# Reordering the down product of a gated feed-forward block: all high parts first, then all low parts

## The chip, the cores and the metric

The kernel runs on one core of a Trainium2 chip. The metric is the time of one execution on the device in microseconds, and the time given for a kernel is the median of its runs. Besides, one execution is recorded by the hardware profiler, and all timelines below are from that one. The engines are named as in the profile: PE (TensorE, matrix products; PEld is its load of the stationary operand), DVE (VectorE), ACT (ScalarE), POOL (GpSimd) and SP (SyncE, which here issues DMAs).

## The reference

One transformer layer over 4 x 2048 = 8192 tokens of 256 numbers, float32: chunked linear attention with a decay and a gate, then a gated feed-forward part with integer weights. Each part is added to its input and normalized.

```python
Q, K, V = x @ W_q.T, x @ W_k.T, x @ W_v.T          # chunks of 32 tokens
S = einsum('bncd,bnkd->bnck', Qc, Kc) * mask       # decay ** (i - j), lower triangle
O = einsum('bnck,bnkd->bncd', S, Vc)
x = layernorm(x + (sigmoid(x @ W_g.T) * O @ W_o.T + x))
h = silu(x @ wg.T) * (x @ wu.T)                    # 768 wide, integer weights / 127
x = layernorm(x + h @ wd.T)
```

## The kernel before

**Tiles.** The 8192 tokens go in 16 blocks of 512 (`TB`), each of four groups of 128 tokens (`NG` = 4). A PSUM bank holds 512 float32 numbers for each partition, that is two groups of 256 features. Eight banks are handed out in turn by `bank(name)`; a bank is free again when its last reader is done.

**Parts.** Products that need more than one pass's precision are split. In the attention part, `token_parts` cuts a tensor into `hi` (ACT), `lo` (POOL: `x_lo` is x minus its high part) and `gap`, which is made later, by `x_gaps()` on DVE: two instructions (line 477), one for each half of the features. `three` (line 524) multiplies hi and lo parts, has ACT scale the bank in place (line 531), and multiplies the gap parts on top. In the feed-forward part the activations `u` are cut into `u_hi` (fp32r, cast on ACT, line 904) and `u_lo` (float16, POOL, line 905), and the integer weights lie ready as `fd_hi` (fp32r) and `fd_lo` (float16). The hidden dimension of 768 is six chunks of 128.

**The down product.** `ffn_down` (line 922) multiplies u by the down weights. For the blocks b = 0 to 12 it calls `project_back`, 48 products of 128 x 128 by 128 x 256: for each of the four groups six high products (one for each chunk) and six low ones, all into the group's half of a bank. `back_terms` turns the order round in every second group, so PE runs high, low, low, high, high, low, low, high. When a bank's two groups are done, `finish`, here `residual` (line 930), is called: DVE adds h to the bank (line 933) and takes the statistics for the norm (`moments`, lines 336 and 337). The last blocks take another path (`chunkwise`, line 953, and line 1313).

**The order of the work.** Every instruction here is issued through `in_turn`: on each engine the instructions run in the order in which the program names them. So where a call stands in the program sets its place in each engine's queue. The loop over b (from line 1101) works on three blocks at once: the feed-forward part of b, the attention output of b + 2, the attention projections of b + 3. Around the down product the order is: PE ends the output product of block b + 2 (`p_o`); DVE adds x to it and takes its statistics (`st_a`, `mv_a`); ACT makes the high part of the next x (`x_hi`), then loads the table for the square root, makes `rstd_h` and, from the block before, `rstd_out` (line 345), and loads the table of silu again; POOL makes `x_lo`. Then comes `ffn_down` with `between`, a function that makes the scale and shift of the norm of h on DVE (`scale_and_shift`, lines 384 to 387: a reciprocal, two multiplications, `minus_h` and `scale_h`, and `shift_h`) and then calls `x_gaps()`. `residual` calls it once, behind the first bank's statistics. After that DVE takes the reciprocal for `rstd_out`.

The next turn of the loop begins with ACT normalizing h (line 424, needs `shift_h`), PE with the gate and up products of chunk 0 (`fg`, `fu`, line 879), ACT with silu of it (`s`, line 888), DVE with `u` (line 899), then four 32 x 32 transposes `sq` (line 831), which 16 DMAs on SP's queue bring to `hT`. PE goes on with chunk 1, the products `p_y` (line 490) of the next x, chunk 2 and the gap products of `p_y`; DVE copies them to `yT` (line 556), and PE takes `yT` in the scores `ps` (line 652).

Of the kernel before, what the change touches and what calls it, by code (L numbers as in the profile page):

```python
# [54 lines left out]
P = 128  # L55
# [4 lines left out]
NG = TB // P  # L60
# [16 lines left out]
def kernel(  # L77
# [15 lines left out]
    nc = tc.nc  # L93
    NT, D = x.shape
# [19 lines left out]
    def in_turn(ins):  # L114
        tc.keep_in_program_order(ins)

    def bank(name):
        return psum.tile([P, TB], F32, tag="ps", name=name)
# [73 lines left out]
    for n in WARM:  # L192
        nc.tensor.matmul(
            pi[:, :n],
            lhsT=nc.const_aps.tensor(0.0, [P, P]),
            rhs=nc.const_aps.tensor(0.0, [P, n]),
            start=True,
            stop=True,
# [129 lines left out]
    def no_moments(name):  # L328
        return small.tile([P, NG, 2], F32, tag="mv", name=f"mv_{name}")

    def moments(r, name, groups=range(NG), order=free, mv=None):

        mv = no_moments(name) if mv is None else mv
        for g in groups:
            st = small.tile([P, 6], F32, tag="st", name=f"st_{name}_{g}")
            order(nc.vector.bn_stats(st, r[:, g, :]))
            order(nc.vector.bn_aggr(mv[:, g, :], st))
        return mv
# [38 lines left out]
    def scale_and_shift(mv, std, kind, name, eng=nc.gpsimd, order=free):  # L377

        on_r, on_dst = kind
        scale, minus, shift = (  # L380
            small.tile([P, NG], F32, tag=tag, name=f"{tag}_{name}")
            for tag in ("scale", "minus", "shift")
        )
        in_turn(nc.vector.reciprocal(std, std))
        for t, sign in ((minus, -1.0), (scale, 1.0)):
            order(eng.tensor_scalar(t, std, sign * on_dst / on_r, None, ALU.mult))
        order(eng.tensor_tensor(shift, mv[:, :, 0], minus, ALU.mult))  # L387
        return scale, shift
# [326 lines left out]
                )  # L715
        return goT

    def back_terms(g, parts, ws):


        pairs = list(zip(parts, ws))[:: -1 if g % 2 else 1]
        return [term for part, w in pairs for term in zip(part, w)]

    def project_back(b, parts, ws, finish, name):


        per = TB // D
        for h in range(NG // per):
            pb = bank(f"{name}_{b}_{h}")
            for j in range(per):  # L730
                g = h * per + j
                terms = back_terms(g, parts, ws)
                for i, (part, w) in enumerate(terms):
                    product = nc.tensor.matmul(  # L734
                        pb[:, j * D : (j + 1) * D],
                        lhsT=part[:, g * P : (g + 1) * P],
                        rhs=w,
                        start=(i == 0),
                        stop=(i == len(terms) - 1),
                    )  # L740
                    in_turn(product)
            finish(slice(h * per, (h + 1) * per), pb)

    def chunked(t):
        return [t[:, k, :] for k in range(t.shape[1])]

    def flat(t, gs):
        return t[:, gs, :].rearrange("p g d -> p (g d)")
# [167 lines left out]
    def early_and_late(parts, ws):  # L916


        hi, lo = (list(zip(part, w)) for part, w in zip(parts, ws))
        return hi[:-2] + lo[:-2], hi[-2:] + lo[-2:]  # L920

    def ffn_down(b, uT, h, between=None, chunkwise=False, amid=None):


        r = work.tile([P, NG, D], F32, tag="r2", name=f"r2_{b}")
        mv = no_moments(f"f{b}")
        made = None
        order = in_turn

        def residual(gs, pb):  # L930

            order(
                nc.vector.scalar_tensor_tensor(
                    flat(r, gs), pb, SCALE**2 / U_UP * H_UP, flat(h, gs), ALU.mult, ALU.add
                )
            )
            nonlocal made
            moments(r, f"f{b}", range(gs.start, gs.stop), order, mv)
            if between is not None and gs.start == 0:
                made = between()  # L940

        ws = [chunked(w) for w in fd]
        if chunkwise:
            per = TB // D
            banks = [bank(f"fdn_{b}_{k}") for k in range(NG // per)]
            for late, terms in enumerate(early_and_late(uT, ws)):
                if late and amid is not None:
                    made = amid()
                for k, pb in enumerate(banks):
                    for i, (part, w) in enumerate(terms):  # L950
                        for j in range(per):
                            g = k * per + j
                            product = nc.tensor.matmul(  # L953
                                pb[:, j * D : (j + 1) * D],
                                lhsT=part[:, g * P : (g + 1) * P],
                                rhs=w,
                                start=late + i + j == 0,
                                stop=True,
                                skip_group_check=True,
                            )  # L960
                            in_turn(product)
                    if late:
                        residual(slice(k * per, (k + 1) * per), pb)
        else:
            project_back(b, uT, ws, residual, "fdn")
        return r, mv, made

    def store(b, r, start=None):
# [4 lines left out]
    def finish(b, r, start=None):  # L973
        layer_norm(r, f"f{b}", on_r=H_UP)
        store(b, r, start)
# [107 lines left out]
    def up_with_cast(b, hT, uT, hc, kind, pieces):  # L1083

        multiply = ffn_up(b, hT, uT, range(hc, hc + 1), held=True)
        if b == 0:
            cast_fd(kind, pieces)
        multiply()

    uT_0 = [], []  # L1090
    mv = out_rest(lambda: up_with_cast(0, hTs[0], uT_0, 0, 0, range(2)))
# [9 lines left out]
    for b in range(NB - 2):  # L1101
# [7 lines left out]
        uT = ([], []) if b else uT_0  # L1109
# [57 lines left out]
        if more:  # L1167
# [15 lines left out]
            def between():  # L1183
                scales = scale_and_shift(
                    mv_h, std_h, of_h, f"h_{b}", nc.vector, in_turn
                )
                if m + 1 < NB:
                    x_gaps()
                return scales

            r_out, mv_out, scales_h = ffn_down(b, uT, hs.pop(b), between)
            if b:
                scales_out = scale_and_shift(mv_before, std_before, of_out, f"out_{b}")
        else:
# [8 lines left out]
            def amid():  # L1203
                return iterated_scale_and_shift(out_rest(), (HALF, 1.0), f"h_{n}")

            r_out, mv_out, scales_h = ffn_down(
                b, uT, hs.pop(b), chunkwise=True, amid=amid
            )
# [6 lines left out]
    per = NG // 2  # L1215
    cols = [slice(i * per * P, (i + 1) * per * P) for i in range(2)]
    uT_last = [], []
    uT = [], []
# [28 lines left out]
    up(last, uT_last, 0, 1)  # L1247
    no_more_splits()
    r_before, mv_before, _ = ffn_down(last - 1, uT, hs[last - 1], chunkwise=True)
    scales_out = iterated_scale_and_shift(mv_before, of_out, f"out_{last - 1}")  # L1250
    up(last, uT_last, 1, KH - 3)
# [3 lines left out]
    for i in range(per):  # L1255
        ffn_up(last, hTs[last], uT_last, range(KH - 2 + i, KH - 1 + i), cols[0])
        g = per + i
# [31 lines left out]
    r = work.tile([P, NG, D], F32, tag="r2", name=f"r2_{last}")  # L1289
# [17 lines left out]
    banks = [bank(f"fdn_{last}_{g}")[:, :D] for g in range(NG)]  # L1307
# [263 lines left out]
```

## Time and profile before

| What | Value |
|---|---|
| median of 3 runs | 489.17 us (489.13 to 489.43) |
| the profiled execution | 489.44 us |
| its span in the profile | 487.8 us |
| granted clock of PE | 0.999 |
| down product of one block (line 734), b = 0 to 12 | 5.43 us, 48 products |
| from one down product to the next | 23.91 us |
| PE, busy share of the span | 99% |
| ACT, DVE, POOL, busy share | 77%, 69%, 58% |

A line of a timeline gives start and length in microseconds, the engine, the line of the kernel, the operation, output <- inputs (buffer numbers left out), the form of output and input, and how many like instructions are taken together. Matrix products overlap, so the length of such a group is more than the distance to the next. A row of stretches gives, behind the stretch and its length, the busy time of each engine with its number of instructions, the granted clock, and the DMA's share and rate.

### The profile page before, as it was taken

How to read it: one execution, taken by the hardware profiler on the slowest of the kernel's cores; microseconds unless marked ns; L12 is line 12 of the kernel's file. 1: busy time of each engine (PE TensorE's matmuls, PEld its weight loads, DVE VectorE, ACT ScalarE, POOL GpSimd, SP SyncE). 2: the span in 40 equal slices, each digit the busy share in tenths (PEclk: the TensorE clock that was granted, in tenths of full speed). 3: DMA queues.
4: the chain of work that ended last, by engine and by line, in shares of the span. 5: the costliest groups of instructions: out<-in, count | busy, mean ns of one | idle time of the engine just before them, and what ended most of it. 6: DMA issues, size and time to landing. Idle time of an engine off the chain costs nothing.

```text
span 487.8 us, 12289 instructions
## 1 busy us (share of the span) xinstructions
PE 481.4 (99%) x4760; PEld 382.3 (78%) x4760; DVE 338.7 (69%) x795; ACT 374.5 (77%) x699; POOL 281.2 (58%) x285
## 2 busy tenths in 40 slices
PE   9999999999999999999999999999999999999995
PEld 5787787887868878687887868878687887868674
DVE  4687958687575876757677575875757677567656
ACT  4878687687877878688687877878688787786845
POOL 3835755555735565464555735566465555657764
PEclk9999999999999999999999999999999999999999
DMA  8820411211403123131411403123132211103102
GB/s 258 253 92 7 131 45 51 80 46 42 133 22 110 44 59 118 31 101 54 118 47 39 134 25 110 45 80 94 27 105 54 79 44 38 53 20 112 35 14 83
DMA packets 43323, 36.99 MB, mean 76 GB/s; under 512 B 4864, under 2 KB 39168, under 8 KB 43264
## 3 DMA queue, kind: packets, MB, share of 16 engines
q1 hardware_dynamic: 42144, 35.28, 24.4%
q10 hardware_dynamic: 1120, 0.92, 0.6%
q8 instruction: 38, 0.62, 0.5%
q14 instruction: 21, 0.17, 0.1%
HBM read 20.45 MB, written 8.39 MB: 59 GB/s over the span
## 4 chain that ended last, share of the span: by engine, by line
PE 98%; DMA 1%; DVE 0%; ACT 0%; issue 0%
PE fg L879 18%; PE fu L879 18%; PE fdn L734 14%; PE p_v L512 9%; PE p_o L512 9%; PE p_y L490 9%; PE p_g L490 9%; PE po L688 4%; PE ps L652 2%; PE fdn L953 2%; PE fdn L1313 1%; PE pg L576 1%; DMA wg<-in_w_gT_dram 1%; PE pa L767 1%; PE pv L618 1%; PE py L597 1%
## 5 line engine op out<-in xcount | busy, mean ns | idle before, releaser
L905 POOL TENSOR_TENSOR u_lo<-u,u_hi 128x512 f16<-128x512 f32 (+1 forms) x98 | 129.4, 1325 | 96.5 <-ACT u_hi L904 95.4
L899 DVE SCALAR_TENSOR_TENSOR u<-fu,s 128x512 f32<-128x512 f32 (+1 forms) x98 | 66.1, 675 | 84.7 <-ACT s L888 82.5
L888 ACT ACTIVATE s<-fg 128x512 f32<-128x512 f32 (+1 forms) x98 | 57.4, 585 | 48.1 <-PE fg L879 48.1
L904 ACT CAST u_hi<-u 128x512 fp32r<-128x512 f32 (+1 forms) x98 | 59.4, 606 | 32.8 <-DVE u L899 32.8
L879 PE MATMUL fg<-hT_hi,fg_hi 128*128 128x512 f32 (+1 forms) x196 | 72.4, 451 | 0.0
L879 PE MATMUL fu<-hT_hi,fu_hi 128*128 128x512 f32 (+1 forms) x196 | 60.5, 390 | 0.0
L879 PE MATMUL fg<-hT_lo,fg_lo 128*128 128x512 f16 (+1 forms) x196 | 58.2, 379 | 0.0
L879 PE MATMUL fu<-hT_lo,fu_lo 128*128 128x512 f16 (+1 forms) x196 | 57.5, 375 | 0.0
L471 POOL TENSOR_TENSOR go_lo<-goT,go_hi 128x512 fp32r<-128x512 f32 x30 | 44.6, 1506 | 18.2 <-ACT go_hi L470 18.2
L477 DVE SCALAR_TENSOR_TENSOR go_gap<-go_hi,goT 128x512 fp32r<-128x512 f32 x30 | 48.2, 1645 | 0.8 <-ACT go_hi L470 0.7
L471 POOL TENSOR_TENSOR x_lo<-xT,x_hi 128x512 fp32r<-128x512 f32 x30 | 37.8, 1283 | 14.6 <-ACT x_hi L470 14.6
L734 PE MATMUL fdn<-fd_hi,u_hi 128*128 128x256 f32 x312 | 44.6, 285 | 0.0
L879 PEld LDWEIGHTS fg<-hT_hi,fg_hi 128*128 128x128 f32 x196 | 35.7, 190 | 10.3
L879 PEld LDWEIGHTS fu<-hT_hi,fu_hi 128*128 128x128 f32 x196 | 36.6, 188 | 8.4
L788 DVE TENSOR_TENSOR h<-p_o,x 128x512 f32<-128x512 f32 x30 | 19.3, 685 | 32.8 <-PE p_o L512 28.9
L734 PEld LDWEIGHTS fdn<-fd_hi,u_hi 128*128 128x128 f32 x312 | 38.9, 188 | 0.3
L734 PE MATMUL fdn<-fd_lo,u_lo 128*128 128x256 f16 x312 | 38.6, 274 | 0.0
L856 POOL TENSOR_TENSOR hT_lo<-hT,hT_hi 128x512 f16<-128x512 f32 x28 | 35.4, 1284 | 4.3 <-ACT hT_hi L855 4.3
L879 PEld LDWEIGHTS <-fu_lo 128*128 128x128 f16 x196 | 19.2, 98 | 22.2
L734 PEld LDWEIGHTS <-u_lo 128*128 128x128 f16 x312 | 28.4, 98 | 3.9
L424 ACT ACTIVATE h<-h,shift_h,scale_h 128x256 f32<-128x256 f32 x52 | 27.0, 589 | 2.2 <-DVE shift_h L387 0.8
L879 PEld LDWEIGHTS <-fg_lo 128*128 128x128 f16 x196 | 13.1, 98 | 19.2 <-issue 12.8
(175 smaller groups left out, 1042.7 us busy)
## 6 DMA issues: line engine op xcount, KB each, us to landing
x<-in_x_dram SPq DMA_DIRECT2D x16, 512.0 KB, 3.9
xT<-in_xT_dram SPq DMA_DIRECT2D x15, 512.0 KB, 4.7
hT<-sq SPq DMA_DIRECT2D x224, 32.0 KB, 1.9
out_dram<-r SPq DMA_DIRECT2D x13, 512.0 KB, 3.3
out_dram<-r SPq DMA_DIRECT2D x7, 128.0 KB, 1.7
fg_int<-in_ffn_gT_dram SPq DMA_DIRECT2D x3, 256.0 KB, 7.9
fu_int<-in_ffn_uT_dram SPq DMA_DIRECT2D x3, 256.0 KB, 7.1
fd_int<-in_ffn_dT_dram SPq DMA_DIRECT2D x3, 256.0 KB, 5.9
```

The source lines that it names most:

```text
L424: nc.scalar.activation(r[:, g, :], r[:, g, :], AF.Identity, bias=shift[:, g : g + 1], scale=scale[:, g : g + 1],)
L471: in_turn(nc.gpsimd.tensor_tensor(lo[:, k, :], t[:, k, :], whole, ALU.subtract))
L477: nc.vector.scalar_tensor_tensor(gap[:, k, :], whole, -WHOLE, t[:, k, :], ALU.mult, ALU.add)
L490: nc.tensor.matmul(pb, lhsT=a[kind][:, k, i * P : (i + 1) * P], rhs=b[kind][:, k, :], start=kind + k == 0, stop=True, skip_group_check=True,)
L512: nc.tensor.matmul(pb[:, j * D : (j + 1) * D], lhsT=b[kind][:, k, g * P : (g + 1) * P], rhs=a[kind][:, k, :], start=kind + k + j == 0, sto ...
L734: product = nc.tensor.matmul(pb[:, j * D : (j + 1) * D], lhsT=part[:, g * P : (g + 1) * P], rhs=w, start=(i == 0), stop=(i == len(terms) - 1),
L856: nc.gpsimd.tensor_tensor(in_order[1], whole, in_order[0].bitcast(F32), ALU.subtract)
L879: product = nc.tensor.matmul(pb, lhsT=w[kind][:, dc, hc * P : (hc + 1) * P], rhs=hT[kind][:, dc, cols], start=(kind == kinds[0] and dc == ...
L888: in_turn(nc.scalar.activation(s, pg, AF.Silu, scale=SCALE / H_UP))
L899: nc.vector.scalar_tensor_tensor(u, pu, U_UP / H_UP, s, ALU.mult, ALU.mult)
L904: in_steady_turn(nc.scalar.copy(hi, u))
L905: in_steady_turn(nc.gpsimd.tensor_tensor(lo, u, hi.bitcast(F32), ALU.subtract))
```

## The change

`project_back` opens both banks at once. It runs chunk by chunk over the high parts of all four groups (24 products), then the low parts of the first bank (chunk by chunk, two groups each), then those of the second bank. When all 48 products stand, it calls `between()`, and only then `finish` for the two banks. `back_terms` is gone. In `ffn_down`, `begin` takes the place of the call inside `residual`. So on DVE the scale and shift of h and the two differences of x come ahead of both residuals and their statistics; before, they stood between the two.

```diff
-    def back_terms(g, parts, ws):
-        pairs = list(zip(parts, ws))[:: -1 if g % 2 else 1]
-        return [term for part, w in pairs for term in zip(part, w)]
-
-    def project_back(b, parts, ws, finish, name):
+    def project_back(b, parts, ws, finish, name, between):
         per = TB // D
+        banks = [bank(f"{name}_{b}_{h}") for h in range(NG // per)]
+        hi, lo = (list(zip(part, w)) for part, w in zip(parts, ws))
+
+        def product(g, part, w, first=False):
+            in_turn(
+                nc.tensor.matmul(
+                    banks[g // per][:, g % per * D : (g % per + 1) * D],
+                    lhsT=part[:, g * P : (g + 1) * P],
+                    rhs=w,
+                    start=first and g % per == 0,
+                    stop=True,
+                    skip_group_check=True,
+                )
+            )
+
+        for i, term in enumerate(hi):
+            for g in range(NG):
+                product(g, *term, first=i == 0)
         for h in range(NG // per):
-            pb = bank(f"{name}_{b}_{h}")
-            for j in range(per):
-                g = h * per + j
-                terms = back_terms(g, parts, ws)
-                for i, (part, w) in enumerate(terms):
-                    product = nc.tensor.matmul(
-                        pb[:, j * D : (j + 1) * D],
-                        lhsT=part[:, g * P : (g + 1) * P],
-                        rhs=w,
-                        start=(i == 0),
-                        stop=(i == len(terms) - 1),
-                    )
-                    in_turn(product)
+            for term in lo:
+                for g in range(h * per, (h + 1) * per):
+                    product(g, *term)
+        between()
+        for h, pb in enumerate(banks):
             finish(slice(h * per, (h + 1) * per), pb)
...
+            moments(r, f"f{b}", range(gs.start, gs.stop), order, mv)
+
+        def begin():
             nonlocal made
-            moments(r, f"f{b}", range(gs.start, gs.stop), order, mv)
-            if between is not None and gs.start == 0:
+            if between is not None:
                 made = between()
...
-            project_back(b, uT, ws, residual, "fdn")
+            project_back(b, uT, ws, residual, "fdn", begin)
```

## The prediction

> **What bounds the kernel.** I read the busy times first, then stretches of time, then each engine's timeline through one block, then the waits.
>
> ```profile
> PE 481.4 (99%) x4760; PEld 382.3 (78%) x4760; DVE 338.7 (69%) x795; ACT 374.5 (77%) x699; POOL 281.2 (58%) x285
> ```
>
> PE is busy all along, the chain of work gives it 98%, and in the list of waits PE waits 1.0 us in all, at the start. (Its loads stand idle 0.37 us before each `ps`, and the list names `yT`; but in block 9 the second copy ended at 232.69, 0.43 us before the load, so that is not what it waited for.) So time changes in two ways only: products follow each other faster or slower, or PE begins to wait. The blocks are nearly alike, 29.34 us each: 5.43 us of down product (`fdn`), 23.91 us of the rest. Block 8's `fdn`, PE's timeline:
>
> ```profile
> 217.60 0.85 PE L734 MATMUL fdn<-fd_hi,u_hi 128*128 128x256 f32 x6
> 218.28 1.49 PE L734 MATMUL fdn<-fd_lo,u_lo 128*128 128x256 f16 x12
> 219.52 1.66 PE L734 MATMUL fdn<-fd_hi,u_hi 128*128 128x256 f32 x12
> 221.02 1.49 PE L734 MATMUL fdn<-fd_lo,u_lo 128*128 128x256 f16 x12
> 222.26 0.93 PE L734 MATMUL fdn<-fd_hi,u_hi 128*128 128x256 f32 x6
> ```
>
> The reader sees the four turns between high and low. Record by record, the low products start 109 ns apart. The high ones start 113 ns apart in the first and last run, 118 ns in the middle one. (The first high product behind a low one is recorded some 0.08 us early.) No product waits. The next product, `fg`, starts at 223.03.
>
> What must keep up is VectorE (DVE), which has no idle time from 217.40 to 228.67. Its timeline, then one line each of ScalarE's (ACT) and GpSimd's (POOL):
>
> ```profile
> 220.74 0.67 DVE L933 SCALAR_TENSOR_TENSOR r<-fdn,h 128x512 f32<-128x512 f32 x1
> ...
> 222.53 0.14 DVE L384 RECIPROCAL rstd_h<-rstd_h 128x4 f32<-128x4 f32 x1
> ...
> 223.00 1.28 DVE L477 SCALAR_TENSOR_TENSOR x_gap<-x_hi,xT 128x512 fp32r<-128x512 f32 x2
> 224.20 0.69 DVE L933 SCALAR_TENSOR_TENSOR r<-fdn,h 128x512 f32<-128x512 f32 x1
> ...
> 226.08 0.66 DVE L899 SCALAR_TENSOR_TENSOR u<-fu,s 128x512 f32<-128x512 f32 x1
> ```
> ```profile
> 220.97 0.30 ACT L345 ACTIVATE rstd_h<-mv_a,eps 128x4 f32<-128x4 f32 x1
> ```
> ```profile
> 219.69 2.52 POOL L471 TENSOR_TENSOR x_lo<-xT,x_hi 128x512 fp32r<-128x512 f32 x2
> ```
>
> Read off: residual 0 with its statistics is 222.53 - 220.74 = 1.79 us; reciprocal, scale and shift 0.47; the two differences 1.20; residual 1 with statistics 1.81. Residual 0 now runs while `rstd_h` is being made (done 221.27) and while POOL makes `x_lo` (until 222.21).
>
> How late may DVE be? Block 1 answers, since there its first `u` comes 4.03 us behind `fg`, not 3.05:
>
> ```profile
> 76.05 1.28 DVE L386 TENSOR_SCALAR scale_h<-rstd_h 128x4 f32<-128x4 f32 x1
> ...
> 80.33 0.69 DVE L899 SCALAR_TENSOR_TENSOR u<-fu,s 128x512 f32<-128x512 f32 x1
> ...
> 84.87 1.28 DVE L556 COPY yT<-p_y 128x512 f32<-128x512 f32 x2
> ```
> ```profile
> 83.38 1.28 PE L490 MATMUL p_y<-x_gap,m_gap 128*128 128x512 f32 x4
> ...
> 86.40 0.76 PE L652 MATMUL ps<-yT,xT 128*32 128x32 f32 x64
> ```
> ```profile
> 76.30:100.21 23.91, 23.91 (x250) 18.40 (x249) 16.41 (x30) 16.23 (x32) 12.15 (x10) 1.00 0.17 46
> ```
>
> Behind `u`, ACT works without a gap (cast u_hi, silu, two scalings of p_y, cast, silu), then DVE makes the third `u` and copies `yT` until 86.15: 5.82 us from `u`'s start. Half of ps needs that second copy, from its ninth product on, 0.06 us after ps starts. The stretch is still 23.91 us, so one us of lateness is free. Little more is.
>
> **The change, part by part.**
>
> *The order on PE.* Nothing is added or removed: 48 products in each of 13 blocks (b = 0 to 12; later blocks use another path). Four turns become two, the second one at the following `fg`. I take 113.5 ns for the high products, as the run behind `p_o` has it now: 24 x 113.5 = 2.72; low 24 x 109.2 = 2.62; 0.01 for entering the low run (its first two starts, 117 and 119 ns) and 0.015 for `fg` behind a low product (as at 448.63). Sum 5.37 against 5.43: **0.055 us saved a block, 0.72 in all**. The other end: all 24 at 118 ns costs 0.045 a block, 0.6 in all. I take 113, since 113 held through eight high products in two alternating groups at 442.32, the nearest row. The Trainium skill ("TensorE: Matmul & The Clock Gate", Back-to-back issue gap) has N/2.4 + 2.5 ns whatever the type, 109.2 ns for 256 columns. The low row agrees and the high row exceeds it. By the page 48 products are 5.24 us, so no order could gain over 0.19 a block, 2.5 in all; the rows, which I use, give 0.72.
>
> *Operands and banks.* Both banks open at once, so the second bank must be free 2.7 us sooner; it held `v`, copied out by 212.90, hidden. The last `u_lo` is wanted later than now, so no wait arises. Bank 0 is read 2.8 us later (223.56), but the eighth bank after it is `fg` of chunk 2 at 228.48: hidden.
>
> *The move on DVE.* Reciprocal, two scalings, shift and two differences pass residual 0 and its four statistics instructions. No DMA is among them, and no queue of SP or POOL is passed. ACT's normalization of h, which waits for the shift, can start 0.1 us sooner, against its table load; worth nothing. Behind the moved steps wait both residuals, then `u`, the transposes `sq` (their 16 DMAs on SP's queue go about 1.2 us later, wanted some 17 us on: hidden), and all ACT work above.
>
> DVE now has nothing to do from 220.74. The reciprocal follows `rstd_h` at 221.27 + 0.09 (as `u` follows its silu) = 221.36, the first scaling at 221.54. Here a rule speaks against the change. The Trainium skill ("SBUF — State Buffer", SBUF: two separate sides) says that VectorE and GpSimd share a port pair as an exclusive lock: a VectorE instruction in a two-port mode, or with two SBUF inputs against a GpSimd one that reads SBUF, waits out the other's whole instruction. The row agrees: `scale_h` takes 1.28 us at 76.05, beside POOL's `x_lo` (until 77.30), and 0.165 as a rule; `go_gap` beside `go_lo` 1.74, `x_gap` alone 0.68. Residual 0 reads PSUM and one SBUF tensor and ran unhindered there. What is moved into its place does need the lock.
>
> So scaling waits for 222.21, the differences start at 222.36, residual 0 at 223.56, residual 1 at 225.36, `rstd_out` at 227.16, `u` at 227.23: **1.15 us later** (226.08), the two holes 0.6 and 0.65. Then 227.23 + 5.82 + 0.05 (a semaphore to PE, as from `p_v` scaled to its product) = 233.10, against ps's ninth product at 233.12 + 0.06 - 0.055 = 233.12. Just in time: **zero** in the ten blocks 3 to 12, with 20 ns to spare. Ends: a gain is excluded, since PE does not wait there now; 0.25 us each if my sum is short by that.
>
> *Block 1.* In block 0 POOL is later: its two `x_lo` run from 74.77 to 77.30. One scaling slips in between them, the other waits to the same end as now, so the differences still start at 77.31. Nothing is won, and residual 0's 1.80 us come on top: `u` at 82.13. ACT's first scaling of p_y now ends 2.33 behind `u` (82.66), then 84.46, so the p_y products go at 84.51, not 83.32. `yT` ends at 86.15 + 1.80 = 87.95, ps's ninth goes at 88.00, not 86.40: **1.60 us** of wait.
>
> *Block 2.* `x_lo` of block 1 ends at 105.19, the differences start at 105.34, not 105.60; `u` is 1.80 - 0.26 = 1.54 late, at 110.21; + 5.87 = 116.08, against 115.76: **0.32 us**.
>
> *The end.* Block 12 has no differences behind it. Its residuals end 0.4 us later, nothing there is near its limit.
>
> **Sum.** -0.72 + 1.60 + 0.32 + 0 = +1.20 us. The profiled execution took 489.44 (span 487.8 and 1.64 around it), so 490.64, span 489.0. It stands 0.27 above the median of the runs, 489.17; so **490.4**. A measurement can tell about 0.2% from no change, 1.0 us (490.15).
>
> **Rivals.** (1) *No lock in the way*, the one that ends not slower: the scalings and differences run at 221.54 beside `x_lo`, `u` is 0.62 late in the usual block, 0.45 in block 1, where ps then waits 0.25. Sum -0.47: 488.7. It decides if block 1's `u` starts before 81.2 (86.40 + 0.72 - 5.87), for then the wait there is less than what the order saves. For it: `minus_h` at 75.97 took its usual 171 ns while POOL worked. Against: `scale_h` behind it. If PE's order also gains nearer the bound of 0.19, it passes into faster, 487.5. (2) *DVE late in every block*: the margin of 20 ns is none; 0.1 to 0.3 us in ten blocks, 1 to 3 us, 491.4 to 493.4. For it: the holes come in each block. (3) *High products at 118 ns*: + 1.3, 491.7. For it: every other run behind a turn, and the `p_v` products, go at 118.
>
> **How the numbers follow.** My forecast 0.5; its own range is 489.6 to 491.2, a third of it below 490.15. Rival 1 0.2, half of it with the larger gain and past 0.2% faster, half within 0.2%; rival 2 0.16; rival 3 0.14. Slower: 0.33 + 0.16 + 0.14 = 0.63, faster 0.1, same 0.27. The range reaches down over rival 1 but for its faster half (0.1) and up to the middle of rival 2 (0.08 beyond): 488.5 to 492.4.
>
> **What would show it.** Right: `fdn` of 48 products in 5.36 to 5.38 us with one turn; DVE idle some 0.6 us before the reciprocal, then a scaling of about 0.7 us; the differences at 222.4; `u` 4.2 us behind `fg`; in block 1 `u` at 5.9 behind `fg`, PE idle before `p_y<-x_gap` and ps there, and the stretch of 23.91 at 25.5. Wrong: ps delayed in blocks 3 to 12 too, or block 1's stretch unchanged.

## The result, and the profile after

The changed kernel takes 490.42 us, the kernel before 489.43 us on the same chips (medians of 13 runs each; the 489.17 shown above are three of them). The ratio is 1.0021, with a 95% interval of 1.0013 to 1.0030: slower by a fifth of a percent.

In the profiled executions the spans are 487.8 and 490.0 us. Of these 2.2 us, 0.96 lie ahead of the first down product (70.87 and 71.83 us), where the two programs are alike; the start differs by as much from one execution to the next. The profiled execution of the changed kernel, at 491.6 us, is also the slowest of its 13 runs. So below I compare the stretch from the first down product to the 14th, which is the first of the other path, and call it the inner stretch. It holds all that was changed: 371.45 us before, **372.67** after, 1.22 longer.

The page of the changed kernel, the busy times and the chain of work that ended last:

```profile
PE 482.2 (98%) x4760; PEld 381.8 (78%) x4760; DVE 345.8 (71%) x795; ACT 370.8 (76%) x699; POOL 281.0 (57%) x285
...
PE 88%; DVE 4%; ACT 4%; SPq 2%; DMA 1%; issue 1%; DVEq 0%; ACTq 0%
```

The chain of the kernel before:

```profile
PE 98%; DMA 1%; DVE 0%; ACT 0%; issue 0%
```

It now runs through DVE, ACT and a DMA for part of its way. Next, PE's timeline through the same down product as in the prediction. (It is the sixth, so of block 5, and `ps` behind it belongs to block 6; the prediction misnumbers them 8 and 9.)

```profile
220.20 2.89 PE L727 MATMUL fdn<-fd_hi,u_hi 128*128 128x256 f32 x24
222.93 2.79 PE L727 MATMUL fdn<-fd_lo,u_lo 128*128 128x256 f16 x24
225.48 0.71 PE L883 MATMUL fg<-hT_hi,fg_hi 128*128 128x512 f32 x2
```

There is one turn from high to low products inside, in place of four. From the second one on, the 24 high products start 113 or 114 ns apart. DVE and POOL beside it:

```profile
223.91 0.18 DVE L384 RECIPROCAL rstd_h<-rstd_h 128x4 f32<-128x4 f32 x1 [0.48 <-ACT rstd_h L345]
224.12 0.72 DVE L386 TENSOR_SCALAR minus_h<-rstd_h 128x4 f32<-128x4 f32 x1
224.76 0.16 DVE L386 TENSOR_SCALAR scale_h<-rstd_h 128x4 f32<-128x4 f32 x1
...
224.96 1.29 DVE L477 SCALAR_TENSOR_TENSOR x_gap<-x_hi,xT 128x512 fp32r<-128x512 f32 x2
226.16 0.68 DVE L937 SCALAR_TENSOR_TENSOR r<-fdn,h 128x512 f32<-128x512 f32 x1
...
227.97 0.66 DVE L937 SCALAR_TENSOR_TENSOR r<-fdn,h 128x512 f32<-128x512 f32 x1
...
229.81 0.66 DVE L903 SCALAR_TENSOR_TENSOR u<-fu,s 128x512 f32<-128x512 f32 x1
```
```profile
222.31 2.50 POOL L471 TENSOR_TENSOR x_lo<-xT,x_hi 128x512 fp32r<-128x512 f32 x2
```

The reader sees two holes: DVE waits 0.48 us for `rstd_h`, then `minus_h`, four numbers in each partition, takes 0.72 us and ends at 224.84, 0.03 behind POOL's `x_lo` (222.31 + 2.50 = 224.81). The reciprocal ahead of it ran beside `x_lo` in 0.18 us. `u` comes 9.61 us behind the start of the down product; before it was 8.48.

Now the first turn of the loop, from block 0's down product to block 1's `ps`, on DVE, POOL and PE:

```profile
76.60 0.18 DVE L384 RECIPROCAL rstd_h<-rstd_h 128x4 f32<-128x4 f32 x1 [1.55 <-ACT rstd_h L345]
76.81 0.42 DVE L386 TENSOR_SCALAR minus_h<-rstd_h 128x4 f32<-128x4 f32 x1
77.14 0.16 DVE L386 TENSOR_SCALAR scale_h<-rstd_h 128x4 f32<-128x4 f32 x1
77.26 1.20 DVE L387 TENSOR_TENSOR shift_h<-mv_a,minus_h 128x4 f32<-128x4 f32 x1
78.39 1.28 DVE L477 SCALAR_TENSOR_TENSOR x_gap<-x_hi,xT 128x512 fp32r<-128x512 f32 x2
...
83.18 0.69 DVE L903 SCALAR_TENSOR_TENSOR u<-fu,s 128x512 f32<-128x512 f32 x1
...
87.72 1.28 DVE L556 COPY yT<-p_y 128x512 f32<-128x512 f32 x2
```
```profile
75.93 2.51 POOL L471 TENSOR_TENSOR x_lo<-xT,x_hi 128x512 fp32r<-128x512 f32 x2
```
```profile
85.56 1.22 PE L490 MATMUL p_y<-x_gap,m_gap 128*128 128x512 f32 x4 [0.93 <-ACT p_y L531]
...
89.05 0.70 PE L652 MATMUL ps<-yT,xT 128*32 128x32 f32 x56 [0.27 <-DVE yT L556]
```

`minus_h` (0.42 us, usually 0.17) and `shift_h` (1.20, usually 0.16) are held here. PE then waits twice, for ACT's scaling of `p_y` and for `yT`; its loads stand idle a little longer than the products. The stretches between the down products of blocks 0 and 1, 1 and 2, 5 and 6, and then the down product of block 4:

```profile
77.11:102.72 25.61, 24.42 (x251) 18.33 (x249) 18.44 (x36) 16.48 (x32) 12.44 (x11) 1.00 0.16 43
108.00:132.30 24.30, 24.20 (x252) 18.61 (x249) 17.06 (x34) 18.00 (x37) 12.07 (x12) 1.00 0.23 65
225.48:249.49 24.01, 24.01 (x251) 18.52 (x249) 16.57 (x34) 17.74 (x36) 12.10 (x12) 1.00 0.24 68
190.82:196.20 5.38, 5.38 (x51) 5.07 (x49) 4.66 (x15) 5.32 (x11) 4.69 (x4) 1.00 0.31 101
```

The usual block is 5.28 + 24.01 = 29.29, against 29.34 before. (It is cut otherwise: the first `fg` behind a low product is recorded early, so 0.1 us passes from the down product to the stretch.) Block 1 lost 1.60 us, block 2 0.29. Block 4's down product took 5.38 us, 0.10 more than the others.

### The profile page after: what moved, and what is told of

Same layout as the page of the kernel before. It is cut to its first block, busy times and chain, and to the rows that moved or that the text cites. A ratio compares the mean times of both kernels' runs of the same rounds, so it can differ in the third digit from the quotient of the medians.

```text
span 490.0 us, 12289 instructions
## 1 busy us (share of the span) xinstructions
PE 482.2 (98%) x4760; PEld 381.8 (78%) x4760; DVE 345.8 (71%) x795; ACT 370.8 (76%) x699; POOL 281.0 (57%) x285
## 4 chain that ended last, share of the span: by engine, by line
PE 88%; DVE 4%; ACT 4%; SPq 2%; DMA 1%; issue 1%; DVEq 0%; ACTq 0%
PE fg L883 16%; PE fu L883 15%; PE fdn L727 12%; PE p_v L512 8%; PE p_o L512 8%; PE p_g L490 8%; PE p_y L490 7%; PE po L688 3%; PE fdn L959 2%; PE ps L652 2%; SPq L842 2%; PE fdn L1319 1%; PE pg L576 1%; DVE u L903 1%; DMA wg<-in_w_gT_dram 1%
## 5 line engine op out<-in xcount | busy, mean ns | idle before, releaser
L883 PE MATMUL fg<-hT_hi,fg_hi 128*128 128x512 f32 (+1 forms) x196 | 73.6, 457 | 0.0
L727 PE MATMUL fdn<-fd_hi,u_hi 128*128 128x256 f32 x312 | 37.6, 276 | 0.0
L727 PEld LDWEIGHTS fdn<-fd_hi,u_hi 128*128 128x128 f32 x312 | 36.5, 188 | 0.0
L727 PE MATMUL fdn<-fd_lo,u_lo 128*128 128x256 f16 x312 | 36.3, 273 | 0.0
L386 POOL TENSOR_SCALAR minus_out<-rstd_out 128x4 f32<-128x4 f32 x12 | 2.7, 221 | 56.8 <-DVE rstd_out L384 56.8
L727 PEld LDWEIGHTS <-u_lo 128*128 128x128 f16 x312 | 29.5, 98 | 3.7
```

Source lines behind the costliest of these rows:

```text
L727: nc.tensor.matmul(banks[g // per][:, g % per * D : (g % per + 1) * D], lhsT=part[:, g * P : (g + 1) * P], rhs=w, start=first and g % per ...
L883: product = nc.tensor.matmul(pb, lhsT=w[kind][:, dc, hc * P : (hc + 1) * P], rhs=hT[kind][:, dc, cols], start=(kind == kinds[0] and dc == ...
```

## The experiments

My theory was that of the prediction: the order on PE saves 0.05 us a block, the move on DVE costs about 2 us in blocks 1 and 2, since the port that DVE shares with POOL holds it up. Rival 1: the new order itself costs, the move is harmless. Rival 2: the loss lies in the program's start. (These two are numbered as in the expectations below; they are not the prediction's rivals.) The table gives, for each kernel, the median and its ratio to the kernel before, then from the traces the stretch from the first to the 14th down product, the stretch behind block 0's down product (with block 1's work), and `u`'s distance from the start of block 0's down product and of a usual one.

| Kernel | median, us | ratio (95%) | 1st to 14th | behind block 0's | u, block 0 / usual |
|---|---|---|---|---|---|
| before | 489.43 | 1 | 371.45 | 23.91 | 9.46 / 8.48 |
| changed | 490.42 | 1.0021 (1.0013 to 1.0030) | 372.67 | 25.62 | 11.35 / 9.61 |
| order alone | 489.99 | 1.0007 (0.9998 to 1.0015) | 371.28 | 24.01 | 9.55 / 9.60 |
| move alone | 490.80 | 1.0030 (1.0017 to 1.0042) | 372.47 | 24.71 | 10.64 / 9.60 |
| without x_lo | 489.28 | 0.9994 (0.9986 to 1.0002) | 371.00 | 24.17 | 9.82 / 9.07 |
| block 0 as before | 489.35 | 0.9997 (0.9989 to 1.0005) | 371.02 | 24.01 | 9.54 / 9.61 |
| blocks 0, 1 as before | 488.96 | 0.9987 (0.9981 to 0.9994) | 370.73 | 24.00 | 9.55 / 9.62 |
| the same, low first | 489.97 | 1.0007 (0.9998 to 1.0015) | 371.91 | 23.92 | 9.55 / 9.62 |
| the same, by groups | 488.79 | 0.9984 (0.9977 to 0.9990) | 370.86 | 24.03 | 9.55 / 9.61 |
| the same, more on DVE | 492.57 | 1.0053 (1.0039 to 1.0067) | 374.60 | 24.98 | 10.63 / 9.96 |

The kernel before had a median of 489.49 beside the next four kernels and 489.69 beside the last four. In these ten traces the first down product starts between 70.5 and 71.8 us, in no order that follows the changes; this can make the medians stray by some tenths from the inner stretch, which comes from one execution of each kernel.

**The order alone.**

```diff
-        between()
         for h, pb in enumerate(banks):
             finish(slice(h * per, (h + 1) * per), pb)
+            if h == 0:
+                between()
```

> The new order of the products, with the scale, shift and differences back between the two residuals. My theory (the order saves some 0.05 us a block, the move on DVE costs some 2 us in blocks 1 and 2): from the first to the last changed product 0.7 us less than before, block 1's stretch after its predecessor's down product back at 24.0 us, time 488.7 (ratio 0.9985). Residual 0 now waits for its bank, about 1.1 us longer than before, so the first u comes some 9.6 us behind the down product's start; that is just in time. Rival 1 (the new order itself costs, the move is harmless): no faster than the changed kernel, 490.4. Rival 2 (the loss is in the start of the program, 0.96 us there in the profiled run): about 490.4 too, with the first down product at 71.8.

Blocks 1 and 2 no longer wait, and `u` comes at 9.60 as foretold. But the time was not: the ratio is 1.0007, not 0.9985, and its interval leaves that out. The inner stretch is only 0.17 us shorter than before, not 0.7. Two things take the rest. Block 1's down product took 5.38 us (0.10 more than usual). And block 13 waits, which I had not seen coming. The stretch behind block 12's down product, and a line of the list of waits in it:

```profile
428.59:443.05 14.46, 14.33 (x131) 9.59 (x129) 9.91 (x27) 10.65 (x21) 10.29 (x17) 1.00 0.11 27
```
```profile
PEld p_o L512 <- POOL go_lo L471: 0.3, 1, 0.3
```

It is 14.01 us in the changed kernel, so 0.45 is lost there. With the shift back behind residual 0, which must now wait until three quarters of the products stand, ACT's normalization of h waits 1.4 us for the shift, and `u` comes at 9.29 and not 8.07. PE's `p_o` products with `go_lo` then start 0.3 to 0.4 us later than in the changed kernel. So in block 12, once the order is new, the move is useful. Rival 1 falls all the same (the order alone is quicker than the change by 1.39 us of inner stretch); rival 2 falls too: this execution started as late as that of the changed kernel (71.77 us), and what tells the two apart is the inner stretch, which leaves the start out.

**The move alone.** The old order of products; the banks' `finish` calls moved behind them, `between()` ahead of both.

```diff
...
         for h in range(NG // per):
             pb = bank(f"{name}_{b}_{h}")
+            banks.append(pb)
...
+        between()
+        for h, pb in enumerate(banks):
             finish(slice(h * per, (h + 1) * per), pb)
...
```

> The old order of the products, with the scale, shift and differences ahead of both residuals. My theory: DVE is as late as in the changed kernel (u at 11.3 us behind the down product of block 0, 10.0 of block 1, 9.6 later), block 1 is some 1.7 longer than before, block 2 some 0.4, the others the same: +2.1 us, 491.5. Rival 1: 489.4, as before. Rival 2: 490.4 or 489.4, with no longer blocks.

The move costs on its own: 1.03 us of inner stretch where 2.1 were expected, ratio 1.0030. Its two places are right, the size in block 1 is not: 24.71 us, 0.8 more than before, not 1.7, and `u` at 10.64, not 11.3. The lines of ACT, of POOL and of DVE in block 0 show why:

```profile
70.94 1.14 ACT L859 CAST hT_hi<-hT 128x512 fp32r<-128x512 f32 x2
```
```profile
74.13 2.51 POOL L471 TENSOR_TENSOR x_lo<-xT,x_hi 128x512 fp32r<-128x512 f32 x2
```
```profile
76.58 1.28 DVE L477 SCALAR_TENSOR_TENSOR x_gap<-x_hi,xT 128x512 fp32r<-128x512 f32 x2
...
81.37 0.69 DVE L903 SCALAR_TENSOR_TENSOR u<-fu,s 128x512 f32<-128x512 f32 x1
```

Here `x_lo` ends 5.91 us behind the down product's start (70.73); in the changed kernel it was 6.61. It follows the cast of `hT_hi`, which waits for the DMAs that bring `hT`: in each of the ten traces the cast starts 0.14 or 0.15 us behind the landing of the last of them. In the changed kernel:

```profile
72.76 1.14 ACT L859 CAST hT_hi<-hT 128x512 fp32r<-128x512 f32 x2 [0.72 <-issue]
```

The cast began 0.21 us behind the start of the down product in the kernel with the move alone, 0.93 in the changed kernel, 0.72 in the one before, 1.47 in the one with more on DVE, and `x_lo` ended 5.7 us behind the cast in all four. So block 1's loss is not one number: it follows the landing of `hT`, which differs from trace to trace.

**Without POOL's x_lo.** The low part of block 3's x serves for all later blocks, so part of the computation is left out; PE's products are the same.

```diff
...
-            in_turn(nc.gpsimd.tensor_tensor(lo[:, k, :], t[:, k, :], whole, ALU.subtract))
+            if not old:
+                in_turn(nc.gpsimd.tensor_tensor(lo[:, k, :], t[:, k, :], whole, ALU.subtract))
...
-                x_parts, x_gaps = token_parts(xTs[m + 1], f"x_{m + 1}")
+                x_parts, x_gaps = token_parts(xTs[m + 1], f"x_{m + 1}", x_parts)
```

> The changed kernel without POOL's x_lo in the loop: the low part of block 3's x is used again for all later blocks, so the output is not the reference's; the products are as many and as long. If DVE's scaling waits for POOL's instruction because of the shared port: the first scaling takes 0.17 us, not 0.72; x_gap starts 4.2 us behind the down product, u 9.05 (not 9.6), and in block 0 u comes at 10.0 and not 11.35, so block 1 loses 0.3 us and not 1.7, block 2 nothing: 489.0. If the move costs through the residuals alone: u in block 0 still past 11, time 490.4.

DVE and ACT in block 0:

```profile
75.28 0.17 DVE L386 TENSOR_SCALAR minus_h<-rstd_h 128x4 f32<-128x4 f32 x1
...
75.56 1.29 DVE L479 SCALAR_TENSOR_TENSOR x_gap<-x_hi,xT 128x512 fp32r<-128x512 f32 x2
...
80.36 0.69 DVE L905 SCALAR_TENSOR_TENSOR u<-fu,s 128x512 f32<-128x512 f32 x1
```
```profile
71.22 1.15 ACT L861 CAST hT_hi<-hT 128x512 fp32r<-128x512 f32 x2 [0.47 <-issue]
```

The first scaling takes 0.17 us, the differences start 5.02 us behind the down product and not 6.56, `u` comes at 9.82 and 9.07. Block 1 loses 0.16 us, block 2 nothing. Nothing but POOL's two instructions for each block is gone, so the wait on them is shown to be the larger part of block 1's loss. Not all of the difference of 1.44 us is theirs, though: in this execution the cast of `hT_hi` began 0.69 us behind the down product, 0.24 sooner than in the changed kernel, and `rstd_h` with it. Less that, the wait on POOL is worth about 1.2 of the 1.60 us, an estimate from these two traces. The rest, some 0.4 us, is left to the two residuals behind the differences and to the late `hT`.

**Block 0 as before, then blocks 0 and 1.** `between()` stands between the residuals in these blocks alone.

```diff
-        between()
+        if b:
+            between()
         for h, pb in enumerate(banks):
             finish(slice(h * per, (h + 1) * per), pb)
+            if b == 0 and h == 0:
+                between()
```

> The changed kernel, but in block 0 alone the scale, shift and differences stand between the residuals. My theory: block 1's wait of 1.6 us is gone, block 2's 0.4 stays: 488.8 to 489.0. If the loss is spread over all blocks or lies in the program's start: 490.3.

The inner stretch falls by 1.65 us to 371.02, and 1.60 of this lies behind block 0, through this one of thirteen calls. Block 2's loss stays (24.30). The median of 489.35 is above the 488.8 to 489.0 expected, and the interval of its ratio does not tell it from the kernel before.

> The changed kernel, but in blocks 0 and 1 the scale, shift and differences stand between the residuals. My theory: no block waits any more, every block from 0 to 12 is 0.05 us shorter than before (29.29 from one down product to the next), 0.7 us in all: 488.8, faster than both kernels. One block may run its high products at the slower pace, 0.1 us. If the move costs in all blocks: 489.4 or more.

With `b > 1` and `b < 2` in place of the two conditions, no block waits any longer. Blocks 0 and 1 with the stretches behind them, then block 5's:

```profile
70.60:75.87 5.27, 5.27 (x50) 4.98 (x49) 4.06 (x12) 4.97 (x8) 4.10 (x4) 1.00 0.31 99
75.87:99.87 24.00, 24.00 (x251) 18.47 (x249) 16.55 (x36) 16.17 (x32) 12.04 (x10) 1.00 0.18 46
99.87:105.25 5.38, 5.38 (x51) 5.08 (x49) 4.08 (x12) 5.33 (x9) 5.00 (x4) 1.00 0.34 102
105.25:129.26 24.01, 24.01 (x252) 18.52 (x249) 16.57 (x37) 18.16 (x37) 12.12 (x12) 1.00 0.24 66
217.12:222.39 5.27, 5.27 (x50) 4.98 (x49) 4.61 (x15) 5.21 (x10) 4.62 (x4) 1.00 0.33 103
222.39:246.40 24.01, 24.01 (x251) 18.52 (x249) 16.59 (x34) 17.78 (x36) 12.09 (x12) 1.00 0.23 68
```

PE is busy through every stretch. The inner stretch is 0.72 us shorter than before, and the kernel, at 488.96 us and a ratio of 0.9987 (0.9981 to 0.9994), beats both the one before and the changed one.

**Low first.** On top of blocks 0 and 1 as before, `hi` and `lo` change places in `project_back`.

```diff
-        for i, term in enumerate(hi):
+        for i, term in enumerate(lo):
...
-            for term in lo:
+            for term in hi:
```

> The kernel with blocks 0 and 1 as before, but with the low parts of all groups first and the high parts after them: as few turns. If the gain comes from high products keeping the pace of 113 ns that they bring from p_o, while behind a low product they run at 118: the high run takes 2.83 us, a block 29.38 us, the whole 0.6 us longer than before, 490.1. If the gain comes from fewer turns alone: 488.8, as with the high parts first.

The number of turns is that of the kernel with high parts first, yet the inner stretch is 1.18 us longer. The down products of block 1 and of block 5:

```profile
101.18:106.53 5.35, 5.35 (x50) 5.09 (x49) 4.21 (x12) 5.30 (x9) 5.00 (x4) 1.00 0.32 103
218.59:224.04 5.45, 5.45 (x50) 5.19 (x49) 4.79 (x16) 5.39 (x11) 4.62 (x4) 1.00 0.30 99
```

In block 5, as in twelve of the thirteen, the high products behind the low ones start 118 ns apart, and a block is 29.38 us, as expected: with fewer turns it is 0.04 us longer than before. So the gain of the change is one of pace, not of turns. But that high products run slower behind a low one is no rule. In block 1 here all 24 start 113 ns apart behind a low one, and so do, in all 13 blocks of the kernel before, the last six of a down product, while the twelve in its middle run at 118.

**Group by group.** Again on top of blocks 0 and 1 as before.

```diff
-        for i, term in enumerate(hi):
-            for g in range(NG):
-                product(g, *term, first=i == 0)
+        for g in range(NG):
+            for i, term in enumerate(hi):
+                product(g, *term, first=i == 0)
```

The low parts likewise.

> The kernel with blocks 0 and 1 as before, but group by group in place of chunk by chunk: 24 high products, six for each group in turn, then 24 low ones. If only turns and pace count: 29.29 us a block, 488.8, the same. If going round the groups chunk by chunk matters for PE (the same moving operand four times, another bank region each time): more than 0.02 us a block apart.

29.29 us a block, an inner stretch of 370.86, and a ratio whose interval covers that of the chunk-wise order. Going chunk by chunk is not what gains.

**More on DVE.**

```diff
                 made = between()
+            extra = small.tile([P, 6], F32, tag="st", name=f"st_extra_{b}")
+            order(nc.vector.bn_stats(extra, h[:, 0, :]))
```

> The kernel with blocks 0 and 1 as before, and one more statistics instruction on DVE (0.43 us, its result unused) in each of the 13 blocks, behind the differences. It tests the edge that I put at 20 ns, and that the traces put at about 0.08 us: the first u comes 10.0 us behind the down product's start, the second copy of yT ends at 15.8, ps's ninth product waits some 0.35 us in each of blocks 2 to 12 (and less in block 1): 3.5 to 4 us more, 492.5. If DVE has more room than I think: 488.8.

3.87 us more of inner stretch than without it, 492.57 us. The stretch behind block 5's down product:

```profile
224.74:249.02 24.28, 24.21 (x252) 18.61 (x249) 17.02 (x35) 17.68 (x36) 12.07 (x12) 1.00 0.23 67
```

A delay of 0.34 us in `u` (9.96 against 9.62) costs 0.27 here, so the room left was some 0.07 us. DVE, 71% busy in the changed kernel, is within a tenth of a microsecond of setting the time of each of these blocks.

That the 3.87 us fall within the 3.5 to 4 expected is partly luck. The ten usual blocks, from block 2's down product to block 12's, make 2.75 of them; 0.99 lie between the down products of blocks 0 and 1, and most of these are not the added instruction's. In this execution `hT` landed latest of all, `x_lo` ended 7.14 us behind block 0's down product's start, `minus_h` was held at its old place too, and the differences, ahead of the added instruction, started 0.75 us later than without it (7.28 and 6.53):

```profile
77.23 0.93 DVE L386 TENSOR_SCALAR minus_h<-rstd_h 128x4 f32<-128x4 f32 x1
```

So the old place is safe in block 0 only while `hT` does not land much later than in the other traces.

## Why the prediction was right

The mechanism was right in its parts: a small gain on PE, nothing in the usual block, and a loss in blocks 1 and 2 where DVE waits for POOL. That 490.4 was forecast and 490.42 measured is closer than it had to be. The kernel before stood 0.26 us above the median I had, so the medians differ by 0.99 us, not 1.20 (the interval of the ratio, 1.0013 to 1.0030, is 0.64 to 1.47 us). In the traces the sum is +1.20 foretold and +1.22 found: 1.60 in block 1, 0.29 in block 2, and 0.67 saved by the order.

- **The order on PE**: -0.055 us a block foretold, 29.34 to 29.29 found. (The down product of 5.36 to 5.38 us is recorded as 5.28, with 0.1 in the stretch behind it.) High products kept 113 ns through the run in twelve of thirteen blocks; in block 4 they ran at 118 throughout, which is rival 3 in one block, 0.10 us. The bound of 0.19 us a block does not follow from the page: the Trainium skill ("TensorE: Matmul & The Clock Gate", Back-to-back issue gap) gives N/2.4 + 2.5 ns for one isolated product, and says that in a stream it counts too much at large N. The float16 rows here, at 109 ns, give the same 0.19 by themselves, as an estimate.
- **The usual block on DVE**: the differences were put at 4.76 us behind the down product's start (222.36 - 217.60) and stand there (224.96 - 220.20); the scaling at about 0.7 and took 0.72; `u` at 9.63 and came at 9.61. The hole before the reciprocal was 0.48, not 0.6: the reciprocal follows ACT's `rstd_h` by 0.03 us, not the 0.09 that I took from `u` and its silu. That changes nothing, since the end of `x_lo` sets what follows.
- **ps just in time**: the room was put at 20 ns and is about 80. The second copy of `yT` ends 15.40 us behind the down product's start, and the load for ps's ninth product goes at 15.53; where it has to wait, it goes 0.05 behind the copy. The copy ends 5.79 us behind `u`, not 5.82 as in block 1 of the kernel before, and `u` itself is 0.02 sooner. Rival 2 came within 0.1 us in each of the ten blocks 3 to 12 and did not occur.
- **Block 1**: 1.60 foretold, 1.60 found, but partly by luck. I took POOL's times from one execution. In that of the changed kernel `x_lo` ended 0.19 us later, in the kernel with the move alone 0.5 earlier. And both scalings slipped in between the two `x_lo`, so that the shift had to wait, not the second scaling; the end is the same. `u` was 0.09 us later than foretold (11.35, not 82.13 - 70.87 = 11.26) and ps went 1.66 us later than in a usual block, but the products of `p_v` behind it won 0.06 of this back.
- **Block 2**: 0.32 foretold, 0.29 found.
- **The end**: right for the change. That the old place would cost 0.45 us there, once the order is new, I had not worked out; it came up only in the run with the order alone.
- **Rival 1**, no lock in the way, falls by `minus_h` at 0.72 us and by the run without `x_lo`. The `minus_h` of 171 ns that spoke for it, at 75.97, had fallen on the change from the first `x_lo` to the second, at 76.04. The rule of the Trainium skill on the shared port ("SBUF — State Buffer", SBUF: two separate sides), which spoke against this change, is what gave its sign. The runs show the wait (0.17 us without `x_lo`, 0.72 beside it), not that a port is what it waits for.

## What to carry to other kernels

An engine can be idle for a third of the time and still have no room at one point of a loop; find the block that runs latest, see what lateness is hidden there, and hold the moved work against that. When work of VectorE is moved, ask what GpSimd does at the new place. Here an instruction that reads PSUM and one SBUF tensor ran beside it freely (0.67 us), and so did a reciprocal of four numbers in SBUF (0.18), while a scaling of the same four waited for it to end (0.72 in place of 0.17). A change can be right for most turns of a loop and wrong for the first ones, and one condition on the block's number then turns a loss of 0.2% into a gain of 0.13%.

## What the runs showed of the hardware that I had not expected

The pace of fp32r products with 256 columns is a state that lasts: 113 or 118 ns from start to start, the same through a run of 24, while float16 ones keep 109. A run of 24 behind `p_o` was mostly at 113, one behind a low product mostly at 118. But block 4 of the changed kernel, block 1 of four others (order alone, without `x_lo`, blocks 0 and 1 as before, by groups) and four blocks of the one with more on DVE were at 118 behind `p_o`, and block 1 of the kernel with low parts first was at 113 behind a low product, as was the last run of six of every block in the kernel before. The first run of six in block 1 of the kernel before and in block 0 of the one with the move alone was at 118 behind `p_o` too. The gap products of `p_o` ahead of a run, at some 113 to 121 ns in these and in blocks of the other kind, do not tell the two apart. What sets the state stays open; it is worth 0.10 us for a down product of 24 high products.
